# Regrouping the score rounds of a fused attention and mixture-of-experts layer

## The chip, the core and the metric

One core of a Trainium2 chip runs the whole layer in one launch. The metric is the device time of that launch in microseconds (us). The engines named here are PE (TensorE, matmuls; PEld is its weight load), DVE (VectorE), ACT (ScalarE), POOL (GpSimd) and SP (the queue that issues nearly all DMAs). [...]

## The reference

Input `x` is 4 batches of 1024 tokens with 256 channels, fp32. The layer is an attention block and an encoder block with routed experts:

```python
# attention: 16 heads of 16, causal, with a linear bias by distance
x = x + attn(layernorm(x))            # softmax(q k^T / 4 + slope * rel, rel <= 0) v, then w_proj
# encoder block on layernorm(x); T is the first axis (4), B the second (1024)
qkv  = u @ in_proj_w.T + in_proj_b
attn = softmax(q k^T / 4) over the 4 entries of the first axis; ctx = attn @ v
h    = layernorm(u + ctx @ out_w.T + out_b)
e    = max of the two best experts' numbers by h @ router_w.T     # 8 experts
moe  = gelu(h @ w1[e].T + b1[e]) @ w2[e].T + b2[e]
x = x + layernorm(h + moe)
```

## The kernel before

The order of the instructions on every engine is written out by the program itself (`manual_schedule`), in `fast_layer`. Three kinds of work are woven together.

**Attention** goes over four chunks of 256 query tokens, each for the four batches. A *unit* is a batch's 256 queries in chunks 0 to 2, and 128 queries in chunk 3: 20 units. A unit has four head groups `g` of four heads, and a head group has one, two, three and two *score rounds* `r` in chunks 0, 1, 2 and 3: 160 rounds, of which chunk 0 has 16, chunk 1 32, chunk 2 48, chunk 3 64. `score` (L871 on) does a round: matmuls of keys by queries with 32 rows each (L884, `sk<-slots`) into two two-bank PSUM tiles of the pool `ps_s`, which has only these two; then ACT takes the exponential of each (L892, `p<-sk`) into two tiles of the pool `probs`, and in the last round of a head group POOL masks both (L902). So the next round's scores need the exponentials of the round before to be done. `weigh` (L908 on) multiplies a round's `p` by the values (L925, `pv<-p,v`) into one PSUM bank; two head groups share it, and then ACT copies it out (L937, L939) and a DMA writes it to DRAM (L941).

**Preparation and closing of units** hangs on numbers of rounds: `turn`, `project_qk` (two halves) and `value` make the keys, queries and values of a unit from the normalised input; `fill_slots` loads a unit's keys and queries from DRAM (in chunk 0 from the SBUF tile `kq`) into `slots`, four DMAs for a head group; `load_sums`, `invert`, `load_y`, `divide` and `project` divide by the softmax's sums and add the projection to `x`.

**Encoder fronts.** `front(i)` is the encoder block up to routing for 128 positions of all four batches: a generator that yields "E" (DVE work), "D" or "d" (TensorE products, the latter not in the slot of the one before), "DQ" (a D that needs the buffer `qkv`) and "P" (as E, a slot later), each with a cost. Eight fronts are run, at most two at a time. `take_E` lets the running fronts do E pieces up to a cost `most`; `take_D` lets them do D pieces up to `D_SLOT`, and holds a D back for one slot where an E of the same front came just before. After six fronts `tabulate_first` makes the table of the first 18 tiles of tokens for the experts; after all eight `tabulate_rest` makes the other 20. A tile's matmuls are `mtp`, `hid` and `oe`.

`E_slot(k)` runs what is due at round k and then `take_E`; `D_slot(p)` runs what is due at the pair p of rounds and then `take_D`. The main loop goes over the pairs: scores of round 2p; an E slot; a D slot; `fill`; another `take_E`; scores of round 2p+1; the weighted sums of all but the last two rounds, so of two; `fill`; an E slot. `probs` has `N_PROBS` = 7 tiles.

After the loop comes the tail: the last weighted sums, the last unit's closing, the rest of the seventh front, the eighth front, and the experts' tiles (`tile_step`, `Experts.advance`), whose gathers can start when a table exists and the attention's buffers are free.

## Time and profile before

| | |
|---|---|
| runs, us | 877.26, 868.71, 877.30 (median 877.26) |
| profiled execution, us | 877.08, of which span 875.3 |
| mean granted TensorE clock | 0.931 |
| PE busy in the span, us | 767.9 (88%), 8981 matmuls |
| DVE | 535.7 (61%) |
| ACT | 393.1 (45%) |
| POOL | 253.1 (29%) |
| score matmuls L884 | 217.8 us busy, 3456 |
| weighted sums L925 | 146.5 us busy, 3456 |
| exponentials L892 | 289.7 us busy, 320 of 937 ns |
| the last weighted sum of the attention ends | at 656.7 us |

The page gives busy time of each engine, the chain of waits that ended last, and the costliest groups of instructions, with the idle time ahead of each and what ended it. Score matmuls of four heads run side by side in four row groups, so their durations (336 ns on the mean) sum to more than the busy time. In a timeline, the time from the start of one block to the start of the next tells more than the durations, as the ends of matmuls are modelled. The granted clock is 1.0 in most of the attention and 0.5 for short stretches.

### The profile page before, as it was taken

To read this page: it belongs to the slowest core of one execution; us is meant where nothing else is said; L and a number is where in the kernel's file an instruction comes from. 1 tells how busy PE (TensorE), PEld (TensorE's weight loads), DVE (VectorE), ACT (ScalarE), POOL (GpSimd) and SP (SyncE) were. 2 spreads that over 40 slices of the span, in tenths; PEclk is the share of its full clock that TensorE was granted. 3 is DMA by queue.
4 is the path that set the end of the run, shared out by engine and by line. 5 is a ranking of instruction groups with operands and counts; after the bars stand their busy time and mean duration, and the time that the engine had idled before them with its cause. 6 is when DMAs were issued, how large, how long until landed. Compare 5 with 4: busy or idle time off the path is not lost.

```text
span 875.3 us, 22574 instructions
## 1 busy us (share of the span) xinstructions
PE 767.9 (88%) x8981; PEld 576.8 (66%) x8981; DVE 535.7 (61%) x1275; ACT 393.1 (45%) x548; POOL 253.1 (29%) x359
## 2 busy tenths in 40 slices
PE   3998889998999999999999989989995997654993
PEld 2776667666666676666777767677773785543882
DVE  7334346339467773866687483793797668682454
ACT  1453436556555755655654554565461223100220
POOL 5432114212111211112121211121122448115685
PEclk9897979999999999999999999999996999865997
DMA  6445454524423333332554343244215563017550
GB/s 203 116 106 162 113 155 129 156 74 154 134 76 107 94 100 124 98 110 79 153 146 142 112 138 120 75 117 140 74 40 161 161 191 119 8 43 240 170 156 30
DMA packets 79108, 105.60 MB, mean 121 GB/s; under 512 B 19928, under 2 KB 59155, under 8 KB 78484
## 3 DMA queue, kind: packets, MB, share of 16 engines
q1 hardware_dynamic: 73548, 89.22, 34.7%
q0 software_dynamic: 4864, 14.16, 5.2%
q8 instruction: 73, 1.20, 0.6%
q10 hardware_dynamic: 584, 0.70, 0.3%
q14 instruction: 39, 0.32, 0.1%
HBM read 67.58 MB, written 35.12 MB: 117 GB/s over the span
## 4 chain that ended last, share of the span: by engine, by line
PE 58%; DVE 16%; issue 10%; DMA 6%; POOL 6%; ACT 2%; SPq 2%; POOLq 0%; DVEq 0%; ACTq 0%
PE sk L884 16%; PE pv L925 10%; PE qkvp L1469 8%; PE qkp L803 5%; PE op L991 3%; PE vp L824 3%; PE ao L1556 2%; DVE pv L1510 2%; POOL given L1647 2%; PE hid L1687 2%; POOL out_dram L1730 2%; PE oe L1703 2%; ACT p L892 2%; DVE pv L1543 1%; DMA yc<-y 1%
## 5 line engine op out<-in xcount | busy, mean ns | idle before, releaser
L892 ACT ACTIVATE p<-sk 128x1024 f32<-128x1024 f32 (+1 forms) x320 | 289.7, 937 | 210.2 <-PE sk L884 197.9
L902 POOL TENSOR_SCALAR_AFFINE_SELECT p<-p 128x512 f32<-128x512 f32 (+1 forms) x160 | 105.6, 663 | 453.2 <-ACT p L892 450.9
L884 PE MATMUL sk<-slots 32*128 32x128 f32 (+1 forms) x3456 | 217.8, 336 | 21.1 <-ACT p L892 16.2
L884 PEld LDWEIGHTS sk<-slots 32*128 32x128 f32 x3456 | 162.3, 191 | 77.7 <-ACT p L892 31.6
L925 PE MATMUL pv<-p,v 128*32 128x128 f32 (+1 forms) x3456 | 146.5, 318 | 0.0
L925 PEld LDWEIGHTS pv<-p,v 128*32 128x32 f32 x3456 | 98.2, 113 | 36.8 <-issue 7.8
L1469 PE MATMUL qkvp<-w_in,ut 128*128 128x512 f32 (+1 forms) x256 | 92.4, 495 | 0.2 <-DVE x L984 0.2
L803 PE MATMUL qkp<-xt,wqk 128*128 128x256 f32 x256 | 66.7, 406 | 0.7 <-ACT xt L793 0.7
L1469 PEld LDWEIGHTS qkvp<-w_in,ut 128*128 128x128 f32 x256 | 44.4, 190 | 31.1 <-issue 25.7
L803 PEld LDWEIGHTS qkp<-xt,wqk 128*128 128x128 f32 x256 | 50.2, 202 | 11.6 <-issue 2.0
L1687 PE MATMUL hid<-mt,w 128*128 128x128 f32 x304 | 49.9, 304 | 6.0 <-DMA w<-in_w_dram 3.0
L1476 DVE COPY qkv<-qkvp 128x264 f32<-128x264 f32 x28 | 12.1, 432 | 68.6 <-PE qkvp L1469 68.6
L1687 PEld LDWEIGHTS hid<-mt,w 128*128 128x128 f32 x304 | 44.2, 208 | 12.8 <-ACT mt L1676 5.6
L1647 POOL DMA_INDIRECT given<-rows,rows x38 | 42.2, 1109 | 33.2 <-DVE who_f L1283 14.4
L1696 ACT ACTIVATE ge<-hid 128x256 f32<-128x256 f32 x38 | 14.6, 383 | 82.6 <-PE hid L1691 44.2
L808 DVE COPY kq<-qkp 128x512 f32<-128x512 f32 x32 | 21.9, 686 | 46.6 <-PE qkp L803 46.3
L1478 ACT COPY qkv<-qkvp 128x512 f32<-128x512 f32 (+1 forms) x36 | 20.2, 562 | 48.5 <-PE qkvp L1469 45.2
L1510 DVE TENSOR_TENSOR pv<-qkv,sc 128x1024 f32<-128x1024 f32 x32 | 39.6, 1241 | 3.9 <-PE ctp L1533 3.7
L1703 PE MATMUL oe<-w,ge 128*128 x152 | 41.8, 400 | 0.1
L1730 POOL DMA_INDIRECT out_dram<-o,out_rows x38 | 39.4, 1037 | 6.9 <-issue 6.9
L1490 DVE TENSOR_TENSOR pr<-qkv 128x1024 f32<-128x1024 f32 x32 | 39.9, 1246 | 0.0
L991 PE MATMUL op<-wp,yc 128*128 128x256 f32 x124 | 34.6, 421 | 5.9 <-DVE yc L979 5.8
(259 smaller groups left out, 1003.9 us busy)
## 6 DMA issues: line engine op xcount, KB each, us to landing
slots<-k SPq DMA_DIRECT2D x128, 80.0 KB
w<-in_w_dram SPq DMA_DIRECT2D x38, 256.0 KB
k<-kq SPq DMA_DIRECT2D x32, 256.0 KB
y<-yt SPq DMA_DIRECT2D x24, 256.0 KB
v<-v SPq DMA_DIRECT2D x20, 288.0 KB
v<-v SPq DMA_DIRECT2D x4, 1152.0 KB
x<-in_x_dram SPq DMA_DIRECT2D x16, 256.0 KB
rows<-x SPq DMA_DIRECT2D x32, 128.0 KB
```

The source lines that it names most:

```text
L803: nc.tensor.matmul(pm[:, k * W:(k + 1) * W], wqk[:, k, cc, half * P:(half + 1) * P], xt[:, cc], start=cc == 0, stop=cc == CC - 1,)
L884: nc.tensor.matmul(ps[h // 2][:, h % 2, width:to], kt[rows_, kb * P:(kb + 1) * P], qt[rows_, off:], start=True, stop=True,)
L892: nc.scalar.activation(pt[:, :, :width], ps[pair][:, :, :width], AF.Exp, scale=1.0 / math.sqrt(D))
L902: nc.gpsimd.affine_select(blocks, blocks, pattern=[[0, 2], [0, size], [1, P]], compare_op=ALU.is_ge, fill=0.0, base=0, channel_multiplier=-1,)
L925: nc.tensor.matmul(pv[h * S:(h + 1) * S, off:], vt[:, kb, at:at + S], pts[h // 2][:, h % 2, at_p:to], start=r == 0 and k == 0, stop=own an ...
L991: nc.tensor.matmul(pm[:, i * C:(i + 1) * C], yc[:, cc, i * P:(i + 1) * P], wp_sb[:, cc], start=cc == 0, stop=cc == CC - 1,)
L1469: nc.tensor.matmul(pq, ut[:, cc, t * P:(t + 1) * P], w_in_sb[:, cc, lo:hi], start=cc == 0, stop=cc == CC - 1,)
L1510: nc.vector.tensor_tensor(pr.rearrange("p s (h d) -> p s h d", d=D), qkv[:, :, 2 * C:3 * C].rearrange("p s (h d) -> p s h d", d=D), sc[:, ...
L1647: nc.gpsimd.indirect_dma_start(out=self.hx, out_offset=None, in_=t.rows_of, in_offset=bass.IndirectOffsetOnAxis(ap=t.rows_[:, self.j:self. ...
L1687: nc.tensor.matmul(ph[:, fc], self.w1[:, cc, fc * P:(fc + 1) * P], mt[:, cc], start=cc == 0, stop=False,)
L1703: nc.tensor.matmul(self.v, ge[:, fc], late["w2"][:, bass.ds(at + fc * C, C)], start=fc == 0, stop=False,)
L1730: ins = nc.gpsimd.indirect_dma_start(out=out.rearrange("t n c -> (t n) c"), out_offset=bass.IndirectOffsetOnAxis(ap=t.table.out_rows[:, t. ...
```

## The change

The loop goes over groups of rounds in place of pairs. Each half of a unit's head groups (two, which share a PSUM bank of sums) is cut into one or two groups of at most four rounds, shifted by one round: a group ends with the first round of the next half. This gives a group of three and then groups of two in chunk 0, of four in chunk 1, of three in chunk 2 and of four in chunk 3. Behind every round of a group but its last there are an E slot, products, loads of `slots` and another `take_E`; behind the last come the weighted sums of all rounds but the last, the loads and an E slot.

`D_slots(k, most)` takes the place of `D_slot(p)`: it runs all products that are due at pairs up to k/2, with a budget of its own: 4.0 up to chunk 3 and 5.3 in it (before: 5.6 for each pair). The E budget in chunk 3 is 3.0 in place of 3.6, for each slot. `probs` has eight tiles. `fill` waits with a unit's loads until the projection that they read has been issued.

```diff
-N_PROBS = 7
+N_PROBS = 8
...
-D_SLOT, E_SLOT, E_LATE = 5.6, 2.5, 3.6
+D_SLOT, D_LATE, E_SLOT, E_LATE = 4.0, 5.3, 2.5, 3.0
...
+    projected = set()
+
     def project_qk(n, half):
...
+        projected.add((n, half))
...
-    def take_D(cost):
+    def take_D(cost, most=D_SLOT):
...
-                if cost and cost + it.cost > D_SLOT:
+                if cost and cost + it.cost > most:
                     break
...
+    def D_slots(k, most):
+        todo = []
+        for p in sorted(of_D):
+            if 2 * p <= k:
+                todo += of_D.pop(p)
+        for _, what in todo:
+            what()
+        return take_D(sum(cost for cost, _ in todo), most)
...
     def fill():
-        while to_fill:
+        while to_fill and (units[to_fill[0][0]][0], to_fill[0][1] // 2) in projected:
             fill_slots(*to_fill.pop(0))

-    for p in range(len(rounds) // 2):
-        most = E_SLOT if p < begins[(NC - 1) * B] else E_LATE
-        score_next(2 * p)
-        E_slot(2 * p, most)
-        D_slot(p)
-        fill()
-        take_E(0.0, most)
-        score_next(2 * p + 1)
-        while len(waiting) > 2:
-            weigh(*waiting.pop(0))
-        fill()
-        E_slot(2 * p + 1, most)
+    groups, since = [], -1
+    for k, (u, g, r) in enumerate(rounds):
+        if g % 2 and r == n_rounds(u) - 1:
+            m = min(k + 1, len(rounds) - 1) - since
+            parts = -(-m // 4)
+            groups += [m // parts + (n < m % parts) for n in range(parts)]
+            since += m
+
+    k = 0
+    for size in groups:
+        for last in (False,) * (size - 1) + (True,):
+            most = E_SLOT if k < 2 * begins[(NC - 1) * B] else E_LATE
+            score_next(k)
+            if not last:
+                E_slot(k, most)
+                D_slots(k, D_SLOT if most == E_SLOT else D_LATE)
+                fill()
+                take_E(0.0, most)
+            else:
+                while len(waiting) > 1:
+                    weigh(*waiting.pop(0))
+                fill()
+                E_slot(k, most)
+            k += 1
     for it in waiting:
         weigh(*it)
```

## The prediction

> **What bounds the kernel now.** I read, in this order: the shares of the chain of waits, a table of busy time by stage, the waits, and the timelines of TensorE and ScalarE inside one stage. The chain first:

> ```profile
> PE 58%; DVE 16%; issue 10%; DMA 6%; POOL 6%; ACT 2%; SPq 2%; POOLq 0%; DVEq 0%; ACTq 0%
> ```

> TensorE holds most of the chain. Next the span cut at the starts of score rounds 16, 48 and 96 (batch chunks 1, 2 and 3), at the end of the last weighted sum, and at a late point of the tail (the eighth front's first context product, `ctp`):

> ```profile
> 91.70:220.60 128.90, 121.13 (x1268) 85.63 (x1264) 65.94 (x150) 70.49 (x91) 28.66 (x39) 0.96 0.44 131
> 220.60:404.10 183.50, 179.79 (x1892) 118.68 (x1888) 121.32 (x267) 105.64 (x130) 31.56 (x42) 1.00 0.35 102
> 404.10:656.70 252.60, 237.34 (x4259) 186.74 (x4255) 175.43 (x380) 140.53 (x176) 49.51 (x76) 0.97 0.41 114
> 656.70:746.00 89.30, 70.98 (x404) 56.00 (x404) 65.53 (x164) 23.17 (x53) 42.12 (x47) 0.89 0.50 155
> ```

> Columns: stretch, length, then busy time of PE, PEld, DVE, ACT, POOL, and the granted PE clock. PE is busy for 94 to 98% of the three chunks. That looks as if nothing were left to gain there, but "busy" contains score matmuls that stand and wait. PE and ACT around two weighted sums:

> ```profile
> 598.08 1.53 PE L884 MATMUL sk<-slots 32*128 32x128 f32 x32
> 599.54 1.13 PE L991 MATMUL op<-wp,yc 128*128 128x256 f32 x4
> ...
> 604.61 1.17 PE L884 MATMUL sk<-slots 32*128 32x128 f32 x32
> 605.72 1.95 PE L925 MATMUL pv<-p,v 128*32 128x128 f32 x64
> 607.60 1.53 PE L884 MATMUL sk<-slots 32*128 32x128 f32 x32
> ```
> ```profile
> 596.39 2.01 ACT L892 ACTIVATE p<-sk 128x1024 f32<-128x1024 f32 x2 [0.87 <-PE sk L884]
> 605.91 2.01 ACT L892 ACTIVATE p<-sk 128x1024 f32<-128x1024 f32 x2 [4.44 <-PE sk L884]
> ```

> The same 32 score matmuls take 1.11 us from their start to the next block's after encoder products (604.61 to 605.72), and 1.46 after weighted sums (598.08 to 599.54). The reason stands on ACT: the two exponentials (2.01 us from 596.39) end at 598.40, the next round's scores start at 598.08, and their second pair of heads needs the buffer of the second exponential. Weighted sums of two rounds (1.88 us) are just too short a cover. At about half of these gaps one more thing delays that exponential:

> ```profile
> ACT p L892: 11.7, 35
> ```

> This line, of who waited for the weighted sums (us, times; tile `p`, 100 to 656 us), is ACT waiting for one of the seven `probs` buffers.

> [...] the clock is 0.50 from 521.8 to 528.6, behind two rounds with no encoder products. [...]

> **The change, part by part.** The changed kernel's order of instructions shows that the groups come as written: 3, then 2s in chunk 0, 4s in chunk 1, 3s in chunk 2, 4s in chunk 3. Between consecutive rounds lies a gap with weighted sums or one for products.

> *Weighted-sum gaps.* Chunks 1 to 3 had 16, 24 and 31; now 8, 16 and 16. The excess of a score block behind one, read from the PE timeline as above, is 0.62, 0.55 and 0.42 us on average: 9.9 + 13.2 + 13.0 = 36.1 us. Behind sums of three or four rounds (2.5 to 3.7 us) the exponentials (1.94) are done. In a group of four the last round needs two buffers that the first sums of the group free: 0.83 to 0.94 + 0.35 (the wait seen on ACT) + 1.94 = 3.1 to 3.2, against 3.3 to 3.7 of sums; a thin cover, so I allow 2 us (0 to 4). **-34.1.** The eighth buffer alone would take only the 11.7 us, mostly the same time. 31 fewer blocks of sums, each about 0.06 dearer than its share (64 matmuls 1.88 us, 128 3.70): **-1.9.**

> *Product gaps.* They rise from 72 to 103 in chunks 1 to 3 for the same products (204 us before, 206 now), so more stay empty or short, and scores wait for ACT there. Price of an empty gap: with none, scores take 2.52 us behind sums in place of 1.46, and the next 1.79 in place of 0.88, so 1.06 + 0.91 = 1.97 (1.5 where the exponentials are 768 wide). A gap takes the larger of this floor and its content + 0.2 (a lone query-key half 1.92, a second behind it 1.73). Contents by rows of the same timeline: query-key half, values or two-block projection 1.73, one-block 0.87, a pair of flips 0.88, `qkvp` 2.72 a sequence, `ao` 1.0, `place` 0.3, `who` 0.5. Summed over the order of instructions: before 54.5 + 82.1 + 104.5 = 241.1 us (7 empty); after 61.7 + 76.3 + 129.5 = 267.5 (18 empty, 12 of them in chunk 3). **+26.4.**

> *Half clock.* Chunk 3 has four half-clock stretches, 17.1 us together. The one at 521.8 cost some 2.4 us (sums 3.15 in place of 1.67, scores 1.94 in place of 1.46, the rest in a stalled block) in 6.8. Chunk 3 keeps as much PE idling as it had (31 us: excess 13 and gap stalls 18.7, against 30), in denser clumps (rounds 107 to 111, 123 to 126, 134 to 139, 150 to 155). I take one more such stretch: **+2** (-2 to +10).

> *VectorE.* Products that need a fresh DVE result (flips, `place`) could before follow only a slot with a weighted sum between; now only one score block (1.1 us) may lie between a slot of 2.5 to 3 us of DVE work and its product. PE waits for DVE little today (100 to 656 us: 7.0 in front of `op`, 5.0 `xtp`, 2.6 `ctp`). About 14 such products, of which half lie in gaps under the floor: **+2** (-3 to +10).

> *Queues.* The same DMAs are issued. In chunk 0 key-query projections come one round later, and `slots` loads with them; SP is the limit there (four `slots` issues take 2.4 us, a unit's some 25 fill its 15 us) and works some 5 us behind, so this hides: **0** (-2 to +4). If it does not, the first scores of a unit wait. POOL's masks lie behind one product gap and earlier sums: 0. ACT and DVE copies of products keep their number: 0.

> *Tail.* At the end of attention the seventh front has its context flipped and the first routing table is made (both lay behind it), some 14 us of DVE and 1.4 of PE. Before, DVE came to the eighth front's statistics 15.5 us after the last sum (672.2 against 656.7). Yet in the new PE order its flips stand behind seven tiles' products, its `qkvp` behind eleven, at 2.69 us a tile (715.27 to 717.96): first tile about 11 us after the last sum (its weights share the DMA with `w2`), last `qkvp` at about 65 (56 before). Then DVE has 9.8 of score products, 3.3 for a tile pair, 1.0 + 0.8 + 1.5 of softmax and 2.4 of products: `ctp` at about 84.5, against 89.3. **-4** (-9 to +5); behind it the order is unchanged.

> Sum: -34.1 - 1.9 + 26.4 + 2 + 2 - 4 = **-9.6 us**, against the profiled execution's 877.08 (span 875.3, 1.8 around it), which is the median of the runs (877.26) within 0.2: **867.5 us**. One of the three runs was at 868.71, so about 1% is what can be told from no change.

> **Rivals.** *One, slower: the slow scores behind sums come from the switch on the array, not from ACT.* Place: each gap of sums. [...] Then only the 31 gaps that vanish save: 8 x 0.62 + 8 x 0.55 + 15 x 0.42 = 15.7, and the sum is +8.8 us, 886; with the clock's dearer half, more. For it: it is seen at nearly every gap, and PEld idles 0.20 there. Against: PEld idles 0.3 behind products too, without the excess, and at 598 the matmuls speed up when the exponential ends. It is slower than before from the point where under some 26 of the 36 us fall away. Chance 0.15.

> *Two, no change: the gain is given back* by half clocks and waits for DVE at their upper ends, +10 where I took +4, and a tail that gains nothing (its PE order puts tiles ahead of the last front): 877. For it: the clumps, and 12 empty gaps in the last chunk. Against: PE's idling there is no longer than before. Chance 0.33.

> That the change does not do what it says is excluded by its order of instructions.

> **How the numbers follow.** Forecast 0.52, its own range 855 to 875 (residual, clock, DVE and tail mostly do not all err the same way). The range to hold 8 in 10 takes in rival two and most of one: 853 to 885. Faster by over 1% (under 868.5): the lower part of the forecast, 867.5 being its middle, and some luck of run to run: 0.5. Slower by over 1% (above 886): half of rival one and the worst of two: 0.17. Within: 0.33.

> **What would show it.** Right: scores behind sums at 1.1 us (0.87 in chunks 1 and 2) from start to next start; the ACT wait for sums off `p` gone from chunk 2; score waits for ACT up from 15.3 + 29.5; attention ending near 651. Wrong: scores behind sums still at 1.4; more than eight half-clock stretches in chunk 3; PE waiting over 15 us for `ctx`, `u` or `hot`; the stretch from the last sum to the last front's `ctp` at 89 or more.

## The result and the profile after

The changed kernel takes **908.44 us** (median of 4, 903.84 to 909.38) against 876.64 (868.71 to 877.30) beside it: ratio **1.0374**, 95% interval 1.0304 to 1.0444. The prediction said 867.5 (853 to 885). The profiled execution took 907.68 us, span 905.9, mean granted clock 0.913.

The shares of the chain of waits, after:

```profile
PE 65%; DVE 15%; issue 7%; DMA 6%; ACT 3%; POOL 3%; SPq 1%; POOLq 0%; DVEq 0%; ACTq 0%
```

PE holds seven points more of a longer chain. Where, the same table by stage shows (start and end of the stretch, length, busy time of PE, PEld, DVE, ACT and POOL with instructions, granted PE clock, DMA share, GB/s):

```profile
101.35:232.57 131.22, 118.08 (x1241) 82.48 (x1241) 65.03 (x149) 69.69 (x90) 25.98 (x38) 0.95 0.40 123
232.57:401.60 169.03, 166.22 (x1853) 109.92 (x1854) 94.41 (x217) 101.02 (x124) 30.44 (x39) 0.99 0.34 108
401.60:689.10 287.50, 257.40 (x4338) 201.92 (x4336) 205.96 (x449) 141.92 (x181) 46.91 (x78) 0.91 0.37 103
```

Against before: chunk 0 (with what lies ahead of it) 101.3 us in place of 91.7, chunk 1 131.2 for 128.9, chunk 2 169.0 for 183.5, chunk 3 **287.5 for 252.6**; the rest, from the attention's end, 216.7 for 218.6. (From its first weight load chunk 3 takes 287.7; the tables below count so.) PE is *busy* 257 of 287 us in chunk 3, 20 us more than before. That is not more work of that size: the clock column fell from 0.97 to 0.91. The clock's own record has chunk 3 at half clock (granted clock 0.5) for 54.6 us in place of 17.1. Of chunk 2's gain, 10.8 us are products that the smaller budget pushed into chunk 3: PE content that moved, not time won.

What the change was to cure is cured. PE's timeline around the sums of four rounds:

```profile
571.03 3.70 PE L928 MATMUL pv<-p,v 128*32 128x128 f32 x128
574.66 1.17 PE L887 MATMUL sk<-slots 32*128 32x128 f32 x32
575.77 0.19 PE L1617 MATMUL place<-hot,lower 128*128 128x32 bf16 x1
```

The 32 score matmuls behind sums now take 1.11 us to the next start, where they took 1.46. What was lost stands in the same timeline a hundred us earlier, at rounds 109 to 112. First PE, then ACT:

```profile
467.18 1.17 PE L887 MATMUL sk<-slots 32*128 32x128 f32 x32
471.83 2.56 PE L887 MATMUL sk<-slots 32*128 32x128 f32 x24 [3.47 <-ACT p L895]
475.27 2.78 PE L887 MATMUL sk<-slots 32*128 32x128 f32 x32 [0.88 <-ACT p L895]
477.98 5.02 PE L928 MATMUL pv<-p,v 128*32 128x128 f32 x112
482.94 0.95 PE L887 MATMUL sk<-slots 32*128 32x128 f32 x24
```
```profile
465.01 1.51 ACT L895 ACTIVATE p<-sk 128x768 f32<-128x768 f32 x2 [0.56 <-PE sk L887]
469.47 0.42 ACT L1504 ACTIVATE sc<-sc 128x256 f32<-128x256 f32 x1 [2.95 <-DVE sc L1502]
469.80 0.57 ACT L832 COPY v<-vp 128x512 f32<-128x512 f32 x1
470.26 0.59 ACT L793 COPY xt<-xtp 128x512 f32<-128x512 f32 x1
470.74 1.95 ACT L895 ACTIVATE p<-sk 128x1024 f32<-128x1024 f32 x2
```

From 467.18 to 477.98 PE has nothing but scores: two product gaps in a row are empty, that is, no product was due in the gap between two rounds. PE waits for the exponentials, and the clock is at half from 471.4 to 481.6. There 24 score matmuls take 2.56 us (0.95 behind the sums at 482.94), part of it half clock and part a wait for the second exponential, which ends at 472.69; 112 sums at half clock, which need 3.19 elsewhere, take 4.96 to the next start. And the exponential of 470.74, whose scores were there at 468.35, stands on ACT behind an encoder front's softmax (`sc`) that waits 2.95 us for DVE. The stretch costs some 9.4 us over its bare matmuls. Of such clumps chunk 3 has four (rounds 109 to 112, 123 to 126, 134 to 139 and 150 to 155).

Two lines of waits (us, times, longest; 100 to 689 us), ACT's and PE's:

```profile
ACT p L895 <- PE pv L928: 62.1, 23, 4.4
```
```profile
PE sk L887 <- ACT p L895: 28.7, 42, 3.5
```

The first was 11.7 us in 35 places. In a group of four the last round's exponential has to wait for the sums to free buffers. It costs little: it fits under 3.7 us of sums, and most scores behind sums run at their bare length. But it shows what bundling does: sums of four rounds cover one pair of exponentials (1.94 us), no more, because `ps_s` lets scores run only one round ahead. The second was 15.3 us in 28 places.

### The profile page after: what moved, and what is told of

It is laid out like the page before. It is cut to its first block, busy times and chain, and to the rows that moved or that the text cites. A ratio compares the mean times of both kernels' runs of the same rounds, so it can differ in the third digit from the quotient of the medians.

```text
span 905.9 us, 22605 instructions
## 1 busy us (share of the span) xinstructions
PE 768.2 (85%) x8981; PEld 575.9 (64%) x8981; DVE 532.2 (59%) x1275; ACT 389.0 (43%) x548; POOL 247.6 (27%) x359
## 4 chain that ended last, share of the span: by engine, by line
PE 65%; DVE 15%; issue 7%; DMA 6%; ACT 3%; POOL 3%; SPq 1%; POOLq 0%; DVEq 0%; ACTq 0%
PE sk L887 17%; PE pv L928 13%; PE qkvp L1472 9%; PE qkp L806 4%; PE hid L1690 4%; PE oe L1706 3%; PE vp L827 3%; ACT p L895 3%; PE ao L1559 3%; PE op L994 3%; DVE pr L1493 2%; DVE sc L1494 2%; PE oe L1710 2%; POOL out_dram L1733 1%; DMA w<-in_w_dram 1%
## 5 line engine op out<-in xcount | busy, mean ns | idle before, releaser
L895 ACT ACTIVATE p<-sk 128x1024 f32<-128x1024 f32 (+1 forms) x320 | 282.9, 936 | 242.6 <-PE sk L887 176.9
L887 PE MATMUL sk<-slots 32*128 32x128 f32 (+1 forms) x3456 | 215.6, 344 | 41.0 <-ACT p L895 29.6
L905 POOL TENSOR_SCALAR_AFFINE_SELECT p<-p 128x512 f32<-128x512 f32 (+1 forms) x160 | 101.5, 638 | 504.3 <-ACT p L895 502.1
L887 PEld LDWEIGHTS sk<-slots 32*128 32x128 f32 x3456 | 157.4, 198 | 98.0 <-ACT p L895 52.6
L928 PE MATMUL pv<-p,v 128*32 128x128 f32 (+1 forms) x3456 | 149.7, 331 | 0.0
L928 PEld LDWEIGHTS pv<-p,v 128*32 128x32 f32 x3456 | 107.3, 119 | 41.5 <-issue 14.6
L1472 PE MATMUL qkvp<-w_in,ut 128*128 128x512 f32 (+1 forms) x256 | 95.2, 502 | 2.1 <-DVE kq L811 2.1
L806 PEld LDWEIGHTS qkp<-xt,wqk 128*128 128x128 f32 x256 | 49.3, 199 | 10.4 <-issue 1.3
L1690 PEld LDWEIGHTS hid<-mt,w 128*128 128x128 f32 x304 | 43.6, 206 | 15.7 <-issue 9.3
L1479 DVE COPY qkv<-qkvp 128x264 f32<-128x264 f32 x28 | 12.1, 431 | 57.2 <-PE qkvp L1472 57.2
L811 DVE COPY kq<-qkp 128x512 f32<-128x512 f32 x32 | 21.9, 686 | 37.0 <-PE qkp L806 36.8
L1564 DVE TENSOR_TENSOR u<-u,ao 128x264 f32<-128x264 f32 x32 | 13.7, 429 | 50.8 <-PE ao L1563 50.2
L1494 DVE TENSOR_REDUCE sc<-pr 128x64 f32<-128x1024 f32 x32 | 39.0, 1220 | 1.1
```

What stands on the lines that cost most here:

```text
L806: nc.tensor.matmul(pm[:, k * W:(k + 1) * W], wqk[:, k, cc, half * P:(half + 1) * P], xt[:, cc], start=cc == 0, stop=cc == CC - 1,)
L887: nc.tensor.matmul(ps[h // 2][:, h % 2, width:to], kt[rows_, kb * P:(kb + 1) * P], qt[rows_, off:], start=True, stop=True,)
L895: nc.scalar.activation(pt[:, :, :width], ps[pair][:, :, :width], AF.Exp, scale=1.0 / math.sqrt(D))
L905: nc.gpsimd.affine_select(blocks, blocks, pattern=[[0, 2], [0, size], [1, P]], compare_op=ALU.is_ge, fill=0.0, base=0, channel_multiplier=-1,)
L928: nc.tensor.matmul(pv[h * S:(h + 1) * S, off:], vt[:, kb, at:at + S], pts[h // 2][:, h % 2, at_p:to], start=r == 0 and k == 0, stop=own an ...
L1472: nc.tensor.matmul(pq, ut[:, cc, t * P:(t + 1) * P], w_in_sb[:, cc, lo:hi], start=cc == 0, stop=cc == CC - 1,)
```

## The experiments

Theory **A**, at the start: empty product gaps and the half clock that they bring make the loss, in chunk 3. Rival **B**: PE waits in front of products for fresh DVE results. Rival **C**, for chunks 0 and 1: DMAs come late from SP's queue. Kernels with other group sizes share an edit: a chunk marked 'P' runs in pairs as before (two rounds kept back), a number is the largest group, and D and E budgets are given by chunk (here as in `c3_only`).

```diff
+    modes = {0: 'P', 1: 'P', 2: 'P', 3: 4}
+    budgets = {0: (5.6, 2.5), 1: (5.6, 2.5), 2: (5.6, 2.5), 3: (5.3, 3.0)}
...
-                while len(waiting) > 1:
+                while len(waiting) > keep_back:
```

### One part alone: the eighth buffer, chunk 3, chunk 0

`probs8` is the kernel before with `N_PROBS = 8`; `c3_only` is shown above; `c0_pairs` is the changed kernel with `modes = {0: 'P', 1: 4, 2: 4, 3: 4}`.

> The kernel before with eight probs tiles in place of seven, nothing else. Theory 'buffers': ACT's 11.7 us of waiting for sums in tile p go, and the second exponential of some 35 rounds is ready earlier, so scores behind sums of 768-wide rounds start sooner: 870 to 874 us. Rival 'sums alone are too short a cover': the exponentials still end at 1.94 us and sums at 1.65 to 1.88, time unchanged at 877.

> Chunks 0 to 2 in pairs with the old budgets (5.6, 2.5), chunk 3 in groups of four with the new ones (5.3, 3.0), eight probs tiles; the tail keeps the new product budget of 4.0. Theory 'clumps and half clock in chunk 3': nearly all of the loss is there, 895 to 902 us, half-clock time in chunk 3 above 40 us. Rival 'the loss comes from chunks 0 to 2 (late slots, VectorE waits)': 875 to 882 us.

> The changed kernel with chunk 0 in the old pairs (products behind even rounds, sums behind odd ones), the rest as changed. Theory 'late slots in chunk 0': round 16 starts near 92 us in place of 101, total 898 to 900 us. Rival 'chunk 0 only shifts waits that come later anyway': total 906 to 908.

`probs8`: 869.73 us, ratio 0.9957 (0.994 to 0.9975). ACT's waits for sums off `p` (7.9 us in chunk 3) are gone and every chunk is as long as it was within 2 us, so those waits were hidden. The profiled tail is 211.6 us in place of 218.6; why, no run here settles.

`c3_only`: 889.23, ratio 1.0173 (1.0124 to 1.0221). Chunk 3 takes 272.3 us against 253.5 in `probs8`, with 44.4 us of half clock against 23.9. Groups of four in chunk 3 alone make about half of the whole loss.

`c0_pairs`: 899.58, ratio 1.0300 (1.0263 to 1.0338). Chunk 0 is back at 91.6 us, but in the profiled execution round 48 starts at 232.2 us, as in the changed kernel (232.6): the loss moved into chunk 1, where DVE idles 9.7 us for a `yc` load and PE then 5.2 for a copy that is queued behind it. So the loss of chunk 0 goes with its grouping, but that alone does not make what is lost up to round 48.

### The half clock

`warm` fills the 15 empty product gaps from round 32 on with matmuls whose result is not used, against the half clock.

```diff
+                if done == 0.0 and k >= 32:
+                    pw = bank(f"warm_{k}")
+                    for n in range(6):
+                        nc.tensor.matmul(pw[:, :P], ident, ident, start=True, stop=True)
```

> The changed kernel with six matmuls of 128x128 by 128 columns (about 1.3 us, result not used) in each of the 15 empty product gaps from round 32 on. Theory 'half clock': [...] half-clock time in chunk 3 falls from 54 us to under 25, total 888 to 898 us although work is added. Rival 'the waits for the exponentials themselves': the clock gains nothing or the added matmuls only fill the wait, total 905 to 912 us.

897.26 us, ratio 1.0282 (1.0239 to 1.0324). Half clock in chunk 3 falls from 54.6 to 27.3 us (expected: under 25), and chunk 3 from 287.7 to 281.7; the other 5 us of the gain lie outside it. So less half clock goes with a shorter chunk 3, but by 6 us only. That the filler takes about the room that the stall had is likely and not shown.

### Fewer empty gaps, later products, smaller groups, another queue

Each is the changed kernel with one edit: `after_q` (in `load_y`, below), `spread` (`D_LATE` 4.4), `hold2` (in `take_D`, below), `c3_two` (`modes` 3: 2, budgets of chunk 3 5.6 and 3.6).

```diff
-            nc.sync.dma_start(
+            queue = nc.gpsimd if u < 12 else nc.sync
+            queue.dma_start(
                 su[:, cc], r_of[u][at].unsqueeze(1).to_broadcast([some, D, width])
             )
-            nc.sync.dma_start(yc[:, cc], heads_of(u)[at, :D])
+            queue.dma_start(yc[:, cc], heads_of(u)[at, :D])
...
-                    if it.slot >= slot[0] - (it.was == "E"):
+                    if it.slot >= slot[0] - 2 * (it.was == "E"):
```

> The changed kernel with one edit: the four loads per unit of what `divide` multiplies (`su`, `yc`) are issued by POOL in place of SP for the first 12 units. Chunks 0 and 1 are 11.9 us longer than before in the changed kernel (101.3 + 131.2 against 91.7 + 128.9), though products and sums in them are the same. Theory SP queue: SP issues without a break up to about 140 us, and PE waits there for `slots` (7.5 + 3.0 us in four and one places) and for `yc` (3.3) because each load stands in line behind others; 2.4 us of issues a unit off SP let the rest come earlier, so round 48 starts at 222 to 229 us in place of 232.6, and the whole is 3 to 10 us shorter (899 to 905). Theory groups: the loss lies in the products' places (empty gaps, cold clock), and round 48 stays at 231 to 234. POOL may wait for the reciprocals' round trip with masks behind it: then round 48 comes later than 234.

> The changed kernel with D_LATE 4.4 in place of 5.3: in chunk 3 the same products (91.2 us of nominal content, 92.0 before the edit) lie in more gaps, 8 stay empty in place of 12, and the sum of max(content + 0.2, floor) falls by 8 us. Theory empty gaps: chunk 3 loses the 8 us and about half as much half clock (54.6 us of half clock fall to 35 or less), so chunk 3 is 272 to 278 us in place of 287.7 and the whole 893 to 899. Theory waits for DVE: what sets chunk 3 is the chain of the encoder fronts between DVE and PE, and products come no earlier by being spread: chunk 3 stays at 284 to 290.

> The changed kernel with products held back two product slots, not one, behind a DVE piece of the same front. Theory waits for DVE: the 10 us by which product blocks of chunks 1 to 3 last longer than before beyond their content are PE standing in front of products whose DVE result is fresh (`ctp` 5 us at 226.7 and 3.6 at 542, `qkvp` at 410); they fall by 5 us or more, and the whole is 902 or less if the empty gaps (13 in chunk 3 in place of 12) do not take it back. Theory empty gaps and clock: no gain, 906 to 912, since PE then waits for ACT in place of DVE.

> The changed kernel with groups of two in chunk 3 and its old budgets there (5.6, 3.6): 29 filled and 3 empty product gaps in place of 35 and 12, 31 gaps with sums in place of 16. Sum of product gaps 101 us in place of 127 (with 5 us of products less, which fall into the tail), behind sums 10 to 13 us more. Theory empty gaps with half clock: half clock in chunk 3 falls from 54.6 to 20 or less, chunk 3 is 258 to 266 us in place of 287.7 (252.6 before the change, plus the 11 us of products that chunk 2 passes on, less 5), and the whole 885 to 892. Theory that groups of two lose the same behind sums: chunk 3 is 275 or more.

| | us | ratio (95%) | chunk 3 | half clock in it | round 48 starts | tail |
|---|---|---|---|---|---|---|
| changed | 908.44 | 1.0374 (1.0304 to 1.0444) | 287.7 | 54.6 | 232.6 | 216.7 |
| after_q | 897.72 | 1.0266 (1.0196 to 1.0336) | 287.4 | 54.6 | 223.4 | 211.8 |
| spread | 894.75 | 1.0227 (1.0157 to 1.0297) | 267.6 | 30.7 | 228.1 | 224.1 |
| hold2 | 894.02 | 1.0212 (1.0133 to 1.0291) | 286.1 | 58.0 | 225.8 | 209.4 |
| c3_two | 900.37 | 1.0311 (1.0232 to 1.0391) | 253.4 | 20.5 | 226.9 | 248.3 |

The intervals of `after_q` and `c3_two` overlap the changed kernel's, so what their edits do is read from the stages, of one execution each.

A holds in chunk 3. Four empty gaps fewer (`spread`) are worth 20 us there, more than expected, with 24 us less of half clock. Groups of two (`c3_two`) bring it to 253.4, below the expected 258 to 266. B falls there: `hold2` leaves chunk 3 at 286.1; its gain lies in the tail and ahead of round 48, where most of it may be chance (below).

The total of `c3_two` hardly moves though, against what was expected: the attention ends at 648.8 us, 40 earlier, and the tail grows by 32. Its windows of chunk 3 and of the tail's start:

```profile
395.40:648.80 253.40, 243.18 (x4291) 190.17 (x4291) 170.79 (x377) 139.49 (x178) 46.98 (x77) 0.96 0.42 115
648.80:740.00 91.20, 56.02 (x351) 46.46 (x349) 67.88 (x165) 15.47 (x40) 34.90 (x37) 0.78 0.43 135
```

PE is busy 56 of 91 us, clock 0.78: the front pieces that chunk 2's budget of 4.0 had pushed on fell behind the attention, with them the first table, so `who`, the products that make it, ran at 672.9 to 682.0 us, where the changed kernel has it at 650.3 to 654.9. The experts' first tile came at 687.3, 38.5 us behind the attention's end and not 12.0 as in the changed kernel. **The attention's end is one of two dates; the other is the table of the first tiles.**

On C: chunks 0 and 1 are the same in `spread` and `c3_two` as in the changed kernel, and round 48 starts there at 228.1 and 226.9. So 232.6 is a late case, the change's loss in these chunks is 6 to 12 us, and `after_q` takes 3.5 to 9 of it. SP's timeline in the changed kernel speaks for C; PE's, below it, waits where it ends:

```profile
123.34 2.13 SPq L858 DMA_DIRECT2D slots<-k  x4
125.53 0.66 SPq L974 DMA_DIRECT2D su<-r  x1
126.24 0.63 SPq L977 DMA_DIRECT2D yc<-y  x1
126.92 0.58 SPq L974 DMA_DIRECT2D su<-r  x1
127.54 0.58 SPq L977 DMA_DIRECT2D yc<-y  x1
128.21 0.40 SPq L819 DMA_DIRECT2D k<-kq  x1
128.66 0.55 SPq L951 DMA_DIRECT2D sums<-y  x1
129.30 1.92 SPq L858 DMA_DIRECT2D slots<-k  x4
```
```profile
133.09 1.19 PE L994 MATMUL op<-wp,yc 128*128 128x256 f32 x2 [3.27 <-issue]
```

SP issues these loads without a pause, 0.4 to 0.7 us each. `op` needs the `yc` of 127.54, by way of a DVE product that starts only at 132.30; the profile puts DVE's 13.7 us ahead of it down to a load of `slots`.

In chunk 0 it is not the number of loads that holds SP up. SP itself stands there for `kq`, DVE's copy of a key-query projection. SP's waits of 23 to 140 us, first after, then before:

```profile
SPq L815 <- DVE kq L811: 7.9, 2, 4.2
```
```profile
SPq L812 <- DVE kq L808: 0.9, 2, 0.5
```

It stands from 51.37 to 55.66 and from 70.89 to 74.68 us, with all later loads in line behind, and PE's longest waits for chunk 0's `slots` end at 58.10 and 77.10. This wait is 7.8 to 8.0 us in every kernel here that has the new groups in chunk 0 (ten), and at most 1.2 in those that have pairs there (seven). Chunk 0 takes 97.4 to 102.4 us in the former and 90.4 to 93.4 in the latter. `after_q` moves other loads (its expectation had SP issuing without a break), so the wait stays at 7.9 us and chunk 0 is still 97.4.

### Group size alone, at equal budgets

`twos_old` is the changed kernel with the old budgets everywhere and groups of two in chunk 3; `fours_old` differs from it by one number, `modes` 3: 4 in place of 2.

> The changed kernel with groups of two in chunk 3 and the budgets of before everywhere (5.6, 2.5, 3.6), also in the tail; chunks 0 to 2 keep their new groups. Unlike c3_two, whose first table fell behind the attention and whose tail came to 248 us, the table's `counts` stand in the attention again. Theory groups of four in chunk 3: chunk 3 is 236 to 250 us (69 us of products in place of 92), with 22 us or less of half clock, round 96 comes later than in the changed kernel since chunk 1 takes 14 us of products more and chunk 2 five, and the attention ends at 650 to 662; with a tail of 209 to 219 the whole is 865 to 878, so all of the change's loss is gone but for chunks 0 and 1 (+5 to +12 against before), which eat the gain behind sums in chunk 2. Theory budgets (4.0 in chunks 0 to 2 made the loss by pushing products late): the same result would follow; what tells is half clock and time of chunk 3 against c3_two's 253 us, which had the late products and groups of two.

> twos_old with one difference: chunk 3 in groups of four, so budgets (5.6, 2.5, 3.6) and chunks 0 to 2 are the same, and half of its gaps with sums become product gaps: 63 product and sum gaps are 31 + 32 in twos_old and 16 + 47 here, 18 product gaps empty in place of 5 (5 us of products more get done before the attention ends). By the prediction's own prices (empty gap 1.97 or 1.5, content + 0.2, 10 us less behind sums, no half clock) chunk 3 would be 241.6 + 29.5 - 10 = 261 us. Theory empties with their own after-effects (half clock, exponentials late behind ACT's other work): each of the 13 more empty gaps costs 2.7 and more instead, half clock is over 45 us (20.5 in twos_old), and chunk 3 is 270 to 285. Theory budgets: chunk 3 within 5 us of twos_old's 241.6 plus the 5 us of products.

895.97 us, ratio 1.0212 (1.0159 to 1.0266), and 922.35, ratio 1.0531 (1.0467 to 1.0596). Chunk 3 of the two, `twos_old` first:

```profile
442.70:684.30 241.60, 225.79 (x4221) 178.87 (x4221) 144.88 (x323) 136.24 (x172) 41.55 (x76) 0.96 0.45 117
```
```profile
439.10:710.40 271.30, 241.87 (x4261) 193.98 (x4261) 157.06 (x359) 137.88 (x173) 45.37 (x77) 0.90 0.38 105
```

Group size alone: +29.7 us, clock 0.96 to 0.90 (half clock 20.5 to 54.6 us). The prediction's prices without half clock gave +19.5. The other 10 us agree with an estimate: the prediction's own price of half clock, 2.4 us in 6.8, times 34.1 us of it is 12. No run parts them from what else stands behind an empty gap. `twos_old` itself missed its range by 18 us: with the old budgets in the new groups, chunk 1 takes 145.9 us (its products take 15.6 us more than before the change) and chunk 2 194.3 with 17.1 of half clock. So the new budgets were a help to the new groups, not the cause of the loss: with the old ones the change is worth 14 us less.

### Repairs, and a better version

`repaired` joins the edits of `after_q`, `spread` and `hold2`. `threes_c2` is `probs8` with `modes = {0: 'P', 1: 'P', 2: 4, 3: 2}` and D budgets 5.6, in chunk 2 5.0 (its pairs in chunk 3 are groups of two, which keep one round of sums back in place of two); `threes_c2_q` adds the edit of `after_q`.

> The changed kernel with the three edits at once that each took time off alone: POOL for `su` and `yc`, D_LATE 4.4, products held back two slots behind DVE pieces. If their gains (before 897.7, 894.8 and 894.0 of 908 to 900) are of different places they add: round 48 at 223, chunks 2 and 3 together 430 to 440, tail 210 to 217, the whole 868 to 885. If groups of four lose by empty gaps and half clock however products lie, chunk 3 stays above 262 and the whole above 880.

> The kernel before with eight `probs` buffers and the new grouping in chunk 2 alone (groups of three; budgets 5.6, in chunk 2 5.0): the version that the runs so far point to. Chunk 2 has products in 28 of 32 product gaps and no loads that SP is late with. Behind sums chunk 2 saves 8 to 9 us (12.0 to 3.5 in the changed kernel); its product gaps sum to 95 us in place of 82, with 5 us more of products in them, so 8 lost; chunk 3 has 6 us of products less and 12 us less of product gaps. Attention ends at 643 to 652, with probs8's tail of 212 the whole is 857 to 866, against 869.7 of probs8. If a group of three also wakes the half clock or waits for DVE as the fours do, chunk 2 and 3 together stay at 304 or more and the whole at 870.

> threes_c2 with the `su` and `yc` loads of the first 12 units issued by POOL. Theory SP queue: in chunks 0 and 1 the kernel before also waits for DMAs (`slots<-kq` 4.7 us, `yc` 4.6 on DVE and 5.4 on PE), so round 48 starts 2 to 5 us earlier than threes_c2's. Rival: SP is late only where the new groups bunch the loads; no difference within 1.5 us, or POOL's masks are held up and round 48 is later.

`repaired`: 893.11, ratio 1.0196 (1.0139 to 1.0254), against an expected 868 to 885. Its attention ends at 651.8 us, 37 earlier than the changed kernel's and 5 earlier than before's. The tail is 240.2. PE's waits from 652 to 785 us:

```profile
PE ctp L1537 <- DVE pv L1514: 17.0, 1, 17.0
PE mtp L1678 <- DMA given<-rows,rows: 14.6, 2, 11.5
```

The gathers (`given`) wait for the first table, whose `who` runs at 663.4 to 668.8 us, and the last front (`ctp`) for DVE. The gains don't add: of the 37 us by which the attention ends earlier, the tail takes back 23.5, and there the fronts are late.

`threes_c2`: 879.49, ratio 1.0067 (1.0045 to 1.0090), against an expected 857 to 866: a miss that shows the mechanism small. Chunk 2 takes 195.5 us against 182.7 in `probs8`, with 10.2 us at half clock where `probs8` has none. Behind sums it gains 5 us (10.7 to 5.6 over the bare matmuls), behind products and in empty gaps it loses 10 (5.9 to 15.7), products stand 3 us more for DVE, and 5 are products from chunk 3. `threes_c2_q`: 879.99, ratio 1.0072 (1.0048 to 1.0096); round 48 starts 3.2 us earlier (217.7 against 220.9), as C expects, and nothing of it is left at the end.

### ACT's queue

`sc_later` is the changed kernel, `sc_later8` is `probs8`, each with the fronts' softmax exponential one slot later:

```diff
-        yield "E", 0
+        yield "P", 0
         nc.scalar.activation(sc, sc, AF.Exp, scale=1.0 / math.sqrt(D))
```

> The changed kernel with one edit: a front's softmax exponential (`sc`, on ACT) is issued one slot later than the DVE pieces that it reads. In the changed kernel ACT waits for that DVE result 7.5 us in four places of chunk 3 (2.95 ahead of the empty gaps at 467 us), with score exponentials queued behind. Theory ACT queue: these waits fall under 2 us, the run of empty gaps there takes 3 us or more less, and chunk 3 is 278 to 284 us in place of 287.7 though it has 15 empty gaps in place of 12. Theory empty gaps and clock: three more empty gaps cost what is won, 286 to 294.

> The kernel before with eight `probs` buffers and the softmax exponential one slot later. ACT waits 5.9 us for `sc` in chunk 3 of probs8. Theory ACT queue: chunks 2 and 3 together are 2 to 6 us shorter than the 436.2 of probs8, the whole 863 to 868. Otherwise 868 to 872: the waits lie in gaps with cover, and this is probs8 again.

907.95 us, ratio 1.0342 (1.0270 to 1.0413), and 870.37, ratio 0.9958 (0.9936 to 0.9981), which is `probs8` again. In `sc_later` the waits for `sc` rose to 13.0 us (one of 10.5), so the edit did not take away what it was to take away. Chunk 3 is 282.1 us, in the range expected of a shorter queue but not by that cause. What ACT's order of work costs in the empty gaps stays open.

**Faster than both kernels** are only `probs8` and `sc_later8`, by 0.4%.

## Why the prediction was wrong, point by point

To set the terms side by side I summed, for chunks 1 to 3, the time from each block's start to the next over its bare content (a round's scores 0.85 to 1.13 us, products and sums at the prediction's rates):

| over bare content, us | before | after | change | predicted |
|---|---|---|---|---|
| scores behind sums | 34.8 | 3.9 | -30.9 | -34.1 |
| scores behind products and in empty gaps | 31.2 | 71.5 | +40.3 | } +26.4 + 2 + 2 = |
| products | 21.9 | 32.3 | +10.4 | } +30.4 |
| sums, and the content itself | | | +1.6 | -1.9 |
| chunk 0 and ahead of it | 91.7 | 101.3 | +9.6 | 0 |
| tail | 218.6 | 216.7 | -1.9 | -4 |

(The rows sum to +29.1 of +30.6; the rest is cut at the stages' bounds. The first two rows are less sure one by one than together: if all that a block of scores behind sums takes too long counts as the first, also where an empty gap follows, they are some -35 and +46.)

**Weighted-sum gaps: right**, mechanism and size. Rival one, that the array's switch makes scores behind sums slow, is refuted: they run at 1.11, 0.87 in chunk 1 and 1.08 in chunk 2, as they do behind products.

**Half clock: the term that failed most.** The prediction took one more stretch in chunk 3, +2 us, and argued that PE idles no longer than before "in denser clumps". The density was the point: of the 3.4 us windows at full clock with PE busy for under 2.0 us, 103 of 120 were followed by half clock (last section). Chunk 3 has nine stretches in place of four, and chunks 1 to 3 have 71.7 us at half clock in place of 27.3. At the prediction's own price (2.4 in 6.8) the 44.4 more are 16 us, an estimate. The runs give other prices: `fours_old` against `twos_old` leaves 10 us for 34 of half clock, `spread` 12 for 24 (chunk 3 -20, where fewer empty gaps alone were to give -8), `warm` 6 for 27, a lower end if its filler takes room itself. So the term is 10 to 22 us by estimate; no run parts it wholly from the empty gaps that bring it. In the traces 165 of 173 returns to full clock follow a window of 3.4 us with PE busy for 3.3 us or more, and PE was not idle where the clock was lost: ahead of six of the nine falls in chunk 3 it was busy for 1.65 to 1.99 of the last 3.4 us (last section).

**Product gaps: right in kind.** With the half clock's 16 taken out, the two rows (gaps and DVE) are some +35 in place of +28.4. The price of an empty gap left out other ACT work ahead of the exponential, as at 469.47; how much of the difference that is, no run shows.

**VectorE's waits: +2 predicted, within its range at best.** Products stand 10.4 us more over their content, part of it half clock. Single cases are large (5.0 us at `ctp` by 226.7), yet `hold2` won less than 2 us in chunk 3. PE's waits for DVE over the attention, from 100 us on, sum to 12.1 us where they were 11.1, without the 3.27 at `op` above. (The prediction gave 7.0, 5.0 and 2.6 us for those before; the trace has 5.0, 3.5 and 2.1.)

**Queues: 0 with -2 to +4, measured +9.6 in chunk 0, and 6 to 12 up to round 48 over the kernels that share these chunks.** The step "works some 5 us behind, so this hides" failed. SP was not behind at the loads of the later projections: it stood 7.9 us in two places until their copies were there, in place of 0.9, with the other loads in line behind. The score rounds were already waiting for loads before (4.7 us), so there was no slack. The fallback that the prediction named, a unit's first scores waiting, is what the trace shows.

**Fewer sum blocks: -1.9, not seen.** What a longer block saves, blocks at half clock took back (4.96 us where 3.19 is usual).

**Tail: -4 predicted, -1.9 measured**; the last front's first context product comes 90.0 us behind the last sum (89.3 before). And it missed that a tail grows by 24 to 32 us when the first table is late (`c3_two`, `repaired`).

Of the signs named as right, three came: the scores behind sums, ACT's wait off `p`, gone from chunk 2 but for one place, and more waits of scores for ACT; the attention's end did not (689 in place of 651). Of those named as wrong, two came: nine half-clock stretches in chunk 3, and the 90.0 us. Not foreseen was a loss of this size: rival two, which named the clock and DVE, priced them at +10 together.

## What to carry to other kernels

A stall of half a microsecond that appears at every gap can be dearer to cure than to keep: work that covers another engine's latency covers it once per gap, so bundling four small covers into one leaves three gaps to whatever other work there is, and here it did not fill them (-31 us behind sums, +51 elsewhere, half clock included). Count not only how many gaps are left empty but how many lie in a row: chunk 3, with four clumps of them, had the matmul clock at half for 54.6 us in place of 17.1. And before valuing an earlier end of a stage, look for the second date that the next stage waits for: here the encoder fronts' table, behind which the tail took back 23.5 of the 37 us of the repair.

## What the hardware showed unexpectedly

The clock was halved without any long pause of PE. It falls nine times in chunk 3 of the changed kernel. Ahead of six of the falls no wait of PE in the last 5 us is longer than 1.2 us, and in the last 3.4 us PE was busy for 1.65 to 1.99. The windows that end at two of them, 584.0 and 601.1 (columns as above; the clock is still at 1.00 in them):

```profile
580.60:584.00 3.40, 1.65 (x32) 1.27 (x32) 3.33 (x4) 2.24 (x3) 0.00 (x0) 1.00 0.27 80
597.70:601.10 3.40, 1.96 (x34) 1.27 (x32) 3.30 (x6) 2.24 (x4) 0.00 (x0) 1.00 0.90 176
```

In the first of them PE has one round of scores alone, 32 matmuls with waits of 1.17 and 0.42 us, and the next round's come 1.02 us behind them.
